# A four-layer graph network on one core: rows padded to 16 bytes, destination tiles in chunks of three at the end, and fusion, loads and stores moved

## The chip, the cores and the metric

One Trainium2 chip; the kernel runs on one of its cores. The metric is device time in microseconds (us) from the first to the last instruction with what lies around them. Three runs of the kernel before gave 3668.65, 3674.61 and 3675.11 us, a median of 3674.61.

## The reference

3327 nodes with 512 features pass through four layers. Every layer normalises its input, clips it at zero, and adds its result to the input. Layers 0 to 2 are graph attention with 8, 4 and 8 heads; layer 1 adds self loops to the mask. Layer 3 averages over neighbours and applies three linear maps.

```python
# layer 0 (layers 1 and 2 alike; 1 with 4 heads of 128)
Wh = jnp.einsum('nd,hdo->hno', x, W)
e = jax.nn.leaky_relu(f1[:, :, None] + f2[:, None, :], negative_slope=ALPHA)
attention = jax.nn.softmax(jnp.where(adj[None] > 0, e, NEG_INF), axis=-1)
out = jax.nn.elu(jnp.einsum('hnm,hmo->hno', attention, Wh))
# layer 3
agg = mask @ x / jnp.maximum(deg, 1.0)
combined = jnp.concatenate([x @ W_self + b_self, agg @ W_nb + b_nb], axis=-1)
out = jax.nn.relu(combined @ W_comb + b_comb)
# every layer
h = jnp.maximum(_layernorm(x, axis=-1), 0.0)
x = x + layer(h, adj, ...)
```

The adjacency matrix is sparse and skewed: its density is about 0.01.

## The kernel before

**Tiles.** The nodes are 26 tiles of 128 rows (the last has 127). Destination tiles are handled in chunks of up to four (`chunks`, `PER`, L64 and L65), so six chunks of four and one of two. Source tiles are loaded in five groups `JG` of 6, 6, 6, 4 and 4 (L67).

**Attention as two masked sums.** The exponential of a leaky ReLU of s1+s2 is one of two products, depending on the sign of s1+s2. So for every head and pair of tiles a gate of zeros and twos is made (L550 on ACT, or L547 on DVE for the tiles in `GP_ON_DVE`), masked by an AND (L556) and turned into its complement by an XOR (L560); TensorE then multiplies each of the two 0/2 masks with one of two "pieces" of the projected features (L588 and L591). To keep float32 accuracy a feature is split into three bf16 parts side by side: 65 columns times 3 is 195. A row of a source tile holds both halves: 196 columns with one column of ones (for the degree), then 195: `AO` is 196 and `HW` 391 in `dims` (L102). Layer 1 has rows of 388 columns for group 0 and float32 pairs of 258 for the other four groups, for which masks are converted first (`real`, L488 and L493). Its rows are not touched by the change.

**Loops.** `attention` (L505) runs over chunks, heads, and passes of two destination tiles; a pass goes over all 26 source tiles. For each head and chunk all pieces are loaded anew (`load_pieces`, L498; L528 in layer 1) by SP. After the passes DVE reduces the sums (L602, L606), scales them and divides (L619 to L626) into tiles `A`, which are finished later: ELU and residual (`finish`, L654: ACT, DVE, POOL), normalisation (`norm`, L280), transposes (`transposed`, L131), projection for the next layer (`project`, L329, or `project_last`, L370, for layer 3), splitting and storing pieces (`pieces`, L298) and sending scores (`send_s1`, L389).

**Hooks.** These steps of finished tiles are stages of a tile (`node_stages`, L397) that `Hooks.run` (L471) slips in after a pass: a new tile after every third pass, in the last chunk after every pass. What is left when the layer ends is drained (L637 to L641). The last tiles of layer 3's first projection are kept in `left` (tiles 22 to 25).

**Fusion.** Layer 3's maps are multiplied together beforehand: `fuse_weights` (L161), four blocks of 128 rows and one product for the biases, at the end of layers 0 and 1, called by `close` after the drain.

**Order.** Buffers rotate (`bufs`): an instruction that writes a buffer waits for the last reader of what was there. Instructions on an engine, and DMAs of a queue, run in the order in which they were placed when the program was built; `after` (L141) asks for a place behind another instruction, without a wait on the chip. That order isn't the order of the lines: the trace shows gates of a new layer on ACT ahead of copies for tiles still being drained. The first passes of a layer leave out the last group of source tiles (L567 to L569), because it contains the drained tiles.

Of the kernel before, what the change touches and what calls it, by code (L numbers as in the profile page):

```python
# [37 lines left out]
P = 128  # L38
# [14 lines left out]
def tile_gnn(ctx: ExitStack, tc: tile.TileContext, x, adj, W0, a01, W1, al, ar, W2, a2,  # L53
# [11 lines left out]
    chunks = [(t, min(PER, NT - t)) for t in range(0, NT, PER)]  # L65
# [29 lines left out]

    xs = [x] + [[dram.tile([n * P, D], F32, name=f"x{l}_{c}") for c, (_, n) in enumerate(chunks)]
# [5 lines left out]
    def dims(l):  # L102

        H = heads[l]
        DA = D // H + 1
        AO = 3 * DA + 1
        return H, DA, AO, (2 * AO - 1 if l != 1 else 2 * AO)

# [38 lines left out]
    gone = []  # L147

# [12 lines left out]
    def fuse_weights(i, wc):  # L161
        w_src, b_src = ((Ws, bs), (Wn, bn))[i]
        b = pre.tile([P, KC], F32, name="bv", bufs=1)
        if i == 0:
            nc.gpsimd.dma_start(bias, bc.partition_broadcast(P))
        with nc.allow_non_contiguous_dma(reason="512 values"):
            nc.gpsimd.dma_start(b, b_src.rearrange("(c p) -> p c", p=P))
        for k in range(KC):
            w = pre.tile([P, D], F32, name="xt")
            nc.gpsimd.dma_start(w, w_src[k * P:(k + 1) * P, :])  # L170
            wT = transposed(w, pre, "hT")
            pw = ps.tile([P, D], F32, name="mm")
            for m in range(KC):
                nc.tensor.matmul(pw, wT[:, m, :], wc[:, m, :], start=(m == 0), stop=(m == KC - 1))
            xo = pre.tile([P, D], F32, name="h")
            nc.scalar.copy(xo, pw)
            nc.gpsimd.dma_start(Xd[i][k * P:(k + 1) * P, :], xo)
        pb = ps.tile([P, D], F32, name="mm")
        for m in range(KC):
            nc.tensor.matmul(pb, b[:, m:m + 1].to_broadcast([P, P]), wc[:, m, :], start=(m == 0), stop=(m == KC - 1))  # L180
        nc.vector.tensor_add(bias, bias, pb)
# [54 lines left out]
    def open_layer(l):  # L236
        L = Layer()
        L.l = l
        if l == 3:
# [40 lines left out]
    def norm(xt, pool):  # L280
# [3 lines left out]
        nc.vector.bn_aggr(mv[:, 0:2], st)  # L284
# [13 lines left out]
    def pieces(L, t, AB, pool, first):  # L298
# [9 lines left out]
        nc.gpsimd.memset(pt[:, :, :, o, 3 * DA:AO] if l == 1 else pt[:, :, o, 3 * DA:AO], 1.0)  # L308
# [14 lines left out]
        if o == two - 1 and l == 1:  # L323
            for a in range(2):
                nc.sync.dma_start(abd[l][g][:, a, :, js, :].rearrange("h p j w -> p h j w"), pt[:, :, a])
        elif o == two - 1:
            stored[t] = nc.sync.dma_start(abd[l][g][:, :, js, :].rearrange("h p j w -> p h j w"), pt).ins.name

    def project(L, t, hT, pool, first):  # L329
# [7 lines left out]
        for f in range(2):  # L337
            pw = (accs if first else ps).tile([P, D // 2 + H], F32, name="acc" if first else "mm")
            for k in range(KC):
                nc.tensor.matmul(pw, hT[:, k, :], L.w[:, k, f, :], start=(k == 0), stop=(k == KC - 1))  # L340
# [13 lines left out]
        if l == 1 and KIND[g] != "b":  # L354
            for f in range(2):
# [5 lines left out]
                nc.sync.dma_start(abd[l][g][hs, :, :, jj, :].rearrange("h a p w -> p h a w"),  # L361
                                  pt.rearrange("p h a s d -> p h a (s d)").bitcast(F32))
# [7 lines left out]
    def project_last(L, t, hT, i):  # L370
# [5 lines left out]
        for k in range(KC):  # L376
            nc.tensor.matmul(pw, hT[:, k, :], L.w[i][:, k, :], start=(k == 0), stop=(k == KC - 1))
        if i == 0:
            y = pre.tile([P, D], F32, name="AB", bufs=1)
            nc.vector.tensor_add(y, pw, bias)  # L380
            nc.sync.dma_start(y1d[c][kk * P:kk * P + n, :], y[:n])
# [7 lines left out]
    def send_s1(L, t, pool, first):  # L389
# [5 lines left out]
        nc.sync.dma_start(s1d[L.l][:, t * P:(t + 1) * P], s1t[:H])  # L395

    def node_stages(L, t, get_x, pool, first=False):  # L397
# [7 lines left out]
        def s1():  # L405
            behind = gone[-1] if gone else None
            q["hT"] = transposed(q["h"], mp, "A", 6, behind) if late else transposed(q["h"], pool, "hT", 2, behind)

# [843 lines left out]
```

## Time and profile before

| what | value |
|---|---|
| profiled execution, its own time | 3671.68 us |
| span of its instructions | 3669.8 us |
| mean granted clock of TensorE | 0.986 |
| PE busy | 3508.7 us (96%) |
| DVE busy | 2651.4 us (72%) |
| ACT busy | 2518.0 us (69%) |
| POOL busy | 589.2 us (16%) |
| DMA | 773.05 MB, 211 GB/s |
| layer 0 attention | 176.9 to 1263.5 us |
| layer 1 attention | 1281.0 to 2156.5 us |
| layer 2 attention | 2184.5 to 3309.4 us |
| aggregation of layer 3 | 3342.6 us to the end |

PE is TensorE's matmuls, PEld its weight loads, DVE the vector engine, ACT the scalar engine, POOL the general-purpose one, SP the engine that issues most DMAs. A row of a group of instructions gives line, engine, operation, tiles written and read, shapes and count, then busy us, mean ns of one (a latency: matmuls overlap), then the engine's idle time before them and what ended it. A row of a stage gives its start and end, its length, busy us of each engine with the count of instructions, then the granted clock, DMA share and rate. A row in order of time gives start, duration, instruction, and in brackets the idle time before it and its releaser.

### The profile page before, as it was taken

Reading aid. Unit: us, or ns where it says so; the run is one execution under the profiler, and the core shown is the slowest. Engines: PE = TensorE matmul, PEld = TensorE weight load, DVE = VectorE, ACT = ScalarE, POOL = GpSimd, SP = SyncE. Lnnn points to the kernel's source line nnn. Section 1 sums busy time; section 2 is a strip of 40 time slices with the busy share of each in tenths; the row PEclk is TensorE's granted clock in tenths of the full one; section 3 lists DMA queues with packets and bytes.
Section 4 is the critical chain, followed back from the end, with each engine's and each line's share of the span. In section 5 each row is a group of like instructions: output and inputs, shape, how many; then the busy total and the mean of one; then the engine's idle time right before and its main releaser. Section 6 shows DMA issues by size and latency. Waiting matters only on the chain. (4 is left out here: it accounts for less than half of the span.)

```text
span 3669.8 us, 78902 instructions
## 1 busy us (share of the span) xinstructions
PE 3508.7 (96%) x31348; PEld 3172.0 (86%) x31348; DVE 2651.4 (72%) x5230; ACT 2518.0 (69%) x4170; POOL 589.2 (16%) x832
## 2 busy tenths in 40 slices
PE   7799999999999899999999979999999999998998
PEld 5599999999999778888888859989898989886886
DVE  7698888888887789888888766767776767672121
ACT  5678787777787779888888656767666767571111
POOL 6501221202010102122223220001010101010000
PEclk9999999999999999999999989999999999999999
DMA  7777677777756877777877876545455554476331
GB/s 210 230 207 226 201 226 212 215 220 224 220 189 215 270 262 262 270 257 249 275 249 261 320 229 188 187 169 189 167 182 167 191 171 171 160 276 238 113 104 51
DMA packets 321402, 773.05 MB, mean 211 GB/s; under 512 B 36037, under 2 KB 143560, under 8 KB 320384
## 3 DMA queue, kind: packets, MB, share of 16 engines
q1 hardware_dynamic: 293920, 707.23, 57.6%
q0 software_dynamic: 27104, 60.69, 6.8%
q8 instruction: 249, 4.08, 0.4%
q14 instruction: 129, 1.06, 0.1%
HBM read 661.25 MB, written 128.68 MB: 215 GB/s over the span
## 5 line engine op out<-in xcount | busy, mean ns | idle before, releaser
L588 PE MATMUL acc<-ab,tht 128*128 128x195 bf16 (+1 forms) x10816 | 1872.8, 248 | 20.9 <-DVE tht L556 14.5
L591 PE MATMUL acc<-ab,gt 128*128 128x195 bf16 (+1 forms) x10816 | 1872.3, 249 | 3.1 <-DVE gt L560 2.3
L550 ACT ACTIVATE gt<-s1b,ks 128x512 fp8e4<-128x512 f32 (+1 forms) x2464 | 1456.5, 677 | 279.0 <-issue 150.4
L588 PEld LDWEIGHTS <-tht 128*128 128x128 fp8e4 x10816 | 1060.0, 98 | 28.0 <-DVE tht L556 15.4
L591 PEld LDWEIGHTS <-gt 128*128 128x128 fp8e4 x10816 | 1052.6, 97 | 26.6 <-issue 14.6
L581 PE MATMUL acc<-ab,t 128*128 128x258 f32 x4160 | 544.6, 289 | 22.7 <-ACT t L493 19.6
L581 PEld LDWEIGHTS acc<-ab,t 128*128 128x128 f32 x4160 | 520.2, 192 | 35.8 <-ACT t L493 23.1
L556 DVE TENSOR_TENSOR tht<-gt,m 128x768 uint32<-128x768 uint32 (+3 forms) x560 | 447.8, 800 | 141.6 <-ACT gt L550 138.8
L560 DVE TENSOR_TENSOR gt<-tht,m 128x768 uint32<-128x768 uint32 (+3 forms) x560 | 447.0, 799 | 8.2
L493 ACT CAST t<-tht 128x1536 fp32r<-128x1536 fp8e4 x208 | 300.7, 1469 | 57.6 <-PE acc L581 47.2
L547 DVE TENSOR_SCALAR gt<-s1b,ns 128x512 fp8e4<-128x512 f32 (+1 forms) x448 | 213.9, 480 | 150.0 <-PE acc L591 138.3
L664 POOL TENSOR_TENSOR xt<-xt,e 128x512 f32<-128x512 f32 x78 | 114.7, 1471 | 1270.8 <-DVE e L663 1230.6
L788 PE MATMUL acc<-y,mf 128*128 128x512 f32 x1352 | 309.8, 391 | 1.3 <-DVE mf L783 1.3
L550 ACT ACTIVATE tht<-s1b,ks 128x512 fp8e4<-128x512 f32 (+1 forms) x504 | 306.9, 679 | 2.0 <-DMA s1b<-s 2.0
L788 PEld LDWEIGHTS acc<-y,mf 128*128 128x128 f32 x1352 | 253.6, 188 | 57.4 <-DVE mf L783 1.7
L606 DVE TENSOR_REDUCE R<-acc 128x130 f32<-128x390 f32 x416 | 214.7, 555 | 81.8 <-PE acc L591 81.7
L584 PE MATMUL acc<-ab,tht 128*128 128x387 bf16 x1248 | 225.5, 329 | 4.6 <-DMA ab<-ab 2.5
L785 ACT CAST mf<-m 128x768 fp32r<-128x768 fp8e4 (+1 forms) x78 | 59.1, 762 | 244.7 <-PE acc L788 232.9
L340 PE MATMUL mm<-w,hT 128*128 128x260 f32 (+1 forms) x832 | 200.3, 393 | 13.2 <-ACT hT L138 10.4
L340 PEld LDWEIGHTS mm<-w,hT 128*128 128x128 f32 x832 | 156.9, 194 | 38.4 <-ACT hT L138 11.2
L584 PEld LDWEIGHTS <-tht 128*128 128x128 fp8e4 x1248 | 118.7, 98 | 81.9 <-DMA ab<-ab 2.9
L319 POOL TENSOR_TENSOR pt<-r 128x520 bf16<-128x520 f32 (+1 forms) x116 | 143.2, 1254 | 266.1 <-DVE r L315 249.3
(132 smaller groups left out, 3138.2 us busy)
## 6 DMA issues: line engine op xcount, KB each, us to landing
ab<-ab SPq DMA_DIRECT2D x336, 586.5 KB
ab<-ab SPq DMA_DIRECT2D x224, 391.0 KB
ab<-ab SPq DMA_DIRECT2D x112, 774.0 KB
ab<-ab SPq DMA_DIRECT2D x112, 516.0 KB
ab<-ab SPq DMA_DIRECT2D x56, 582.0 KB
s1b<-s SPq DMA_DIRECT2D x120, 256.0 KB
m<-mask SPq DMA_DIRECT2D x72, 384.0 KB
ab<-pt SPq DMA_DIRECT2D x40, 516.0 KB
```

Of the source, the lines that this page charges most:

```text
L340: nc.tensor.matmul(pw, hT[:, k, :], L.w[:, k, f, :], start=(k == 0), stop=(k == KC - 1))
L493: (nc.scalar.copy if KIND[g] == "s" else nc.vector.tensor_copy)(t[:, :k1 - k0, :nj], th[a][g][:, k0:k1])
L547: nc.vector.tensor_scalar(gv[:, :, jj, :], s1v, L.ns2[:, j, h:h + 1], 2.0, op0=ALU.is_gt, op1=ALU.mult, saturate=False)
L550: nc.scalar.activation(gv[:, :, jj, :], s1v, AF.Relu, bias=L.ks2[:, j, h:h + 1], scale=BIG, saturate=False)
L556: nc.vector.tensor_tensor(pu, gu, mu, ALU.bitwise_and)
L560: nc.vector.tensor_tensor(gu, pu, mu, ALU.bitwise_xor)
L581: mm = nc.tensor.matmul(acc[k][:, :2 * DA], thr[g][:, k - ks[0], jj, :], ab[a][g][:, jj, :], start=(j == 0), stop=(j == NT - 1), skip_grou ...
L584: mm = nc.tensor.matmul(acc[k][:, :3 * DA], th[a][g][:, k, jj, :], ab[a][g][:, jj, :3 * DA], start=(j == 0), stop=(j == NT - 1), skip_grou ...
L588: nc.tensor.matmul(acc[k][:, :3 * DA + o], th[0][g][:, k, jj, :], ab[0][g][:, jj, :3 * DA + o], start=(j == 0), stop=False, skip_group_che ...
L591: mm = nc.tensor.matmul(acc[k][:, AO - o:HW], th[1][g][:, k, jj, :], ab[0][g][:, jj, AO - o:HW], start=False, stop=(j == NT - 1), skip_gro ...
L606: nc.vector.tensor_reduce(R[:, k], v.rearrange("p a (s d) -> p a d s", s=3), AX.X, ALU.add)
L788: nc.tensor.matmul(acc[k], mf[:, jj, :], y2[g][:, jj, s, :], start=(j0 + jj == 0 and s == 0), stop=(j0 + jj == NT - 1 and s == 1))
```

## The change

- The last six destination tiles are two chunks of three instead of four and two.
- In layers 0 and 2 a half row (`AO`) is rounded up to a multiple of 8 columns, 200, and the row (`HW`) is twice that, 400. The columns 195 to 199 of both halves are filled with ones. The degree is summed from two columns of the accumulator.
- The pieces of layers 1 and 2 are stored by stage s3 instead of s2 (`to_store`); their scores are sent through POOL's queue instead of SP's.
- Tiles `A` have 8, 6 and 8 buffers in layers 0, 1 and 2 instead of 6, 5 and 6, and layer 1's gate tiles 11 instead of 12.
- In the last head of a layer the x rows of the last chunk are loaded into `A` buffers by POOL, and the biases and the first two weight blocks of the fusion are loaded.
- Two blocks of the fusion and its biases come ahead of the drain, two behind it. The additions behind the kept projections come after the drain.
- In the last chunk a new tile is taken up after every second pass.

```diff
-    chunks = [(t, min(PER, NT - t)) for t in range(0, NT, PER)]
+    chunks = [(0, 4), (4, 4), (8, 4), (12, 4), (16, 4), (20, 3), (23, 3)]
...
+    A_BUFS = [8, 6, 8]
...
-        AO = 3 * DA + 1
-        return H, DA, AO, (2 * AO - 1 if l != 1 else 2 * AO)
+        AO = -(-(3 * DA + 1) // 8) * 8 if l != 1 else 3 * DA + 1
+        return H, DA, AO, 2 * AO
...
-    def fuse_weights(i, wc):
...
+    class Fusion:
+        def __init__(self, i, wc):
+            self.i, self.wc, self.w = i, wc, {}
+            self.w_src, self.b_src = ((Ws, bs), (Wn, bn))[i]
+        def load(self, k, behind):
+            self.w[k] = pre.tile([P, D], F32, name="xt")
+            after(nc.gpsimd.dma_start(self.w[k], self.w_src[k * P:(k + 1) * P, :]), behind)
+        def block(self, k, behind):
+            w = self.w.pop(k)
+            wT = transposed(w, pre, "hT", 2, behind)
             pw = ps.tile([P, D], F32, name="mm")
             for m in range(KC):
+                nc.tensor.matmul(pw, wT[:, m, :], self.wc[:, m, :], start=(m == 0), stop=(m == KC - 1))
+            nc.scalar.copy(w, pw)
+            nc.gpsimd.dma_start(Xd[self.i][k * P:(k + 1) * P, :], w)
...
-        nc.gpsimd.memset(pt[:, :, :, o, 3 * DA:AO] if l == 1 else pt[:, :, o, 3 * DA:AO], 1.0)
+        nc.gpsimd.memset(pt[:, :, :, o, 3 * DA:AO] if l == 1 else
+                         pt[:, :, o].rearrange("p h (a w) -> p h a w", a=2)[..., 3 * DA:AO], 1.0)
...
+        elif first and o == two - 1:
+            stored[t] = nc.sync.dma_start(abd[l][g][:, :, js, :].rearrange("h p j w -> p h j w"), pt).ins.name
         elif o == two - 1:
-            stored[t] = nc.sync.dma_start(abd[l][g][:, :, js, :].rearrange("h p j w -> p h j w"), pt).ins.name
+            L.to_store.append((abd[l][g][:, :, js, :].rearrange("h p j w -> p h j w"), pt))
...
-        nc.sync.dma_start(s1d[L.l][:, t * P:(t + 1) * P], s1t[:H])
+        (nc.sync if first else nc.gpsimd).dma_start(s1d[L.l][:, t * P:(t + 1) * P], s1t[:H])
...
             if L.l != 3:
+                for to, pt in L.to_store:
+                    nc.sync.dma_start(to, pt)
+                L.to_store = []
                 send_s1(L, t, pool, first)
...
+                if last and h == H - 1:
+                    for k in range(nt):
+                        x_last[t0 + k] = load_x(l, t0 + k, mp, "A", A_BUFS[l], behind=gone[-1])
+                    fusion = close()
+                    if fusion:
+                        fusion.load_biases()
+                        fusion.load(0, gone[-1])
+                        fusion.load(1, gone[-1])
...
-                    pt = mp.tile([P, PER * JM * P], FP8, name="tht", bufs=12 if l == 1 else 7)
+                    pt = mp.tile([P, PER * JM * P], FP8, name="tht", bufs=11 if l == 1 else 7)
...
-                                    mm = nc.tensor.matmul(acc[k][:, AO - o:HW], th[1][g][:, k, jj, :],
-                                                     ab[0][g][:, jj, AO - o:HW], start=False, stop=(j == NT - 1),
+                                    mm = nc.tensor.matmul(acc[k][:, AO:AO + 3 * DA + o], th[1][g][:, k, jj, :],
+                                                     ab[0][g][:, jj, AO:AO + 3 * DA + o], start=False, stop=(j == NT - 1),
...
-                                nc.vector.tensor_copy(deg2[:n, t0 + k:t0 + k + 1], acc[k][:n, 3 * DA:AO])
+                                nc.vector.tensor_reduce(deg2[:n, t0 + k:t0 + k + 1],
+                                                        acc[k][:n, 3 * DA:AO + 3 * DA + 1:AO], AX.X, ALU.add)
...
-                        hooks.run(1 if last else 3, hook, 2 if hook % 2 and c == 0 or hook % 3 == 0 and c else 1)
+                        hooks.run(2 if last else 3, hook, 2 if hook % 2 and c == 0 or hook % 3 == 0 and c else 1)
...
         hooks.run(1, 0, 0)
-        run_left()
+        fusion = close()
+        if fusion:
+            for k in range(2):
+                fusion.block(k, gone[-1])
+            fusion.biases(gone[-1])
+        adds = run_left()
         hooks.drain()
-        close()
-        run_left()
+        for add in adds:
+            add()
+        if fusion:
+            for k in range(2, KC):
+                fusion.load(k, gone[-1])
+                fusion.block(k, gone[-1])
+        for add in run_left():
+            add()
...
+    def load_x(l, t, pool, *name, behind=None):
+        n = pn(t)
+        xt = pool.tile([P, D], F32, name=name[0], bufs=name[1])
...
+        ld = (nc.gpsimd if behind else nc.sync).dma_start(xt[:n], x_rows(l, t))
```

## The prediction, made before the changed kernel was run

> **What bounds the kernel now.** I read the costliest groups, then busy time stage by stage, then the order of time in the places where TensorE stood still. The chain that ended last reaches only into the final aggregation (PE 8% of the span) and says nothing of the rest. The two groups that cost most, from the page:
>
> ```profile
> L588 PE MATMUL acc<-ab,tht 128*128 128x195 bf16 (+1 forms) x10816 | 1872.8, 248 | 20.9 <-DVE tht L556 14.5
> L591 PE MATMUL acc<-ab,gt 128*128 128x195 bf16 (+1 forms) x10816 | 1872.3, 249 | 3.1 <-DVE gt L560 2.3
> ```
>
> Half of the span is these 21,632 matmuls of 195 columns (layers 0 and 2). Busy time by stage, in this order: layer 0 chunks 1 to 5, its last chunk, the passage to layer 1; layer 1 chunks 1 to 5, its last chunk, the passage to layer 2; layer 2 chunks 1 to 5, its last chunk, the passage to the aggregation:
>
> ```profile
> core 0: us, PE busy (x) PEld busy (x) DVE busy (x) ACT busy (x) POOL busy (x), PEclk, DMA share, GB/s
> ...
> 338.00:1168.00 830.00, 821.53 (x9196) 808.11 (x9195) 683.37 (x1356) 648.53 (x1115) 137.30 (x205) 1.00 0.70 212
> 1168.00:1263.50 95.50, 89.18 (x925) 85.72 (x922) 75.96 (x203) 79.18 (x196) 13.70 (x20) 1.00 0.88 289
> 1263.50:1307.00 43.50, 32.98 (x117) 19.80 (x116) 23.91 (x53) 36.22 (x63) 12.11 (x22) 0.88 0.69 240
> ...
> 1416.00:2071.50 655.50, 636.46 (x4588) 559.42 (x4587) 558.74 (x1015) 540.44 (x749) 163.42 (x178) 0.98 0.76 258
> 2071.50:2156.50 85.00, 75.00 (x502) 62.22 (x500) 62.10 (x138) 53.41 (x92) 26.44 (x31) 0.98 0.95 335
> 2156.50:2212.60 56.10, 35.66 (x147) 22.78 (x147) 29.94 (x51) 33.51 (x61) 16.12 (x23) 0.79 0.65 198
> ...
> 2352.00:3212.00 860.00, 860.00 (x8727) 779.47 (x8725) 603.01 (x1184) 575.55 (x945) 66.01 (x100) 1.00 0.51 174
> 3212.00:3309.40 97.40, 94.38 (x900) 81.84 (x897) 71.48 (x189) 69.75 (x165) 15.98 (x21) 1.00 0.77 267
> 3309.40:3342.60 33.20, 25.01 (x58) 11.03 (x57) 9.42 (x23) 9.31 (x14) 7.84 (x13) 0.85 0.75 303
> ```
>
> TensorE is the bound: length less PE busy is 8.5, 6.3, 10.5, 19.0, 10.0, 20.4, 0.0, 3.0 and 8.2 us. So time is won by shorter matmul steps, or out of these gaps. The last chunks (two tiles) load as many pieces as full ones: DMA share 0.88 and 0.95 against 0.70 and 0.76. In the passages the granted clock is 0.88, 0.79 and 0.85. The passage to layer 2, in order of time:
>
> ```profile
> 2166.53 1.12 PE L134 MATMUL tp<-ident,h 128*128 128x128 f32 x4 [10.00 <-ACT h L289]
> ...
> 2171.63 1.26 POOL L664 TENSOR_TENSOR xt<-xt,e 128x512 f32<-128x512 f32 x1 [6.00 <-DMA xt<-x]
> ...
> 2175.52 1.33 ACT L550 ACTIVATE gt<-s1b,ks 128x512 fp8e4<-128x512 f32 x2 [9.04 <-DMA s1b<-s]
> ...
> 2176.76 0.56 ACT L138 COPY hT<-tp 128x512 f32<-128x512 f32 x1
> ...
> 2177.37 3.01 PE L340 MATMUL mm<-w,hT 128*128 128x264 f32 x6 [9.73 <-ACT hT L138]
> ```
>
> TensorE waits 10.0 us for the first tile's normalisation and 9.7 us for a copy queued on ACT behind gates that wait for a row of scores. A gap of the kind that repeats in layer 1, chunks 1 to 5:
>
> ```profile
> 1718.82 1.14 ACT L317 COPY pt<-AB 128x520 bf16<-128x520 bf16 x2
> ...
> 1719.87 1.47 ACT L493 CAST t<-tht 128x1536 fp32r<-128x1536 fp8e4 x1
> ...
> 1721.38 0.86 PE L581 MATMUL acc<-ab,t 128*128 128x258 f32 x5 [3.44 <-ACT t L493]
> ```
>
> **The change, part by part.**
>
> *Padded rows.* I took each step from one L588/L591 start to the next: 21,364 lie between 80 and 92 ns, mean 85.67, and they are sorted. Layer 1's matmuls of 387 columns step 163.3 ns at the shortest, these of 195 step 83.3: 192 columns more take 80.0 more, 2.4 columns per ns, so 195 alone would be 81.3 and 83.3 is 200. The 196 columns of layer 0's first head take the same 83.3. It looks as if whole groups of 8 elements (16 bytes) were read. Rows lie 391 elements apart, 7 past a multiple of 8, so the start moves with j. The second matmul of a pair starts 391j+196 in: at j=4, 10, 16 a multiple of 8, and it takes 83.8; at j=3, 9, 15 one past, 83.8 to 85; elsewhere 87 to 88. Layer 1's 387-column matmuls take 168.3 for the first of a pair at odd j (4 past) and 163.3 at even j. One row does not fit: the first matmul of the second tile of a pair takes 83.4 wherever it starts. With rows of 400 and halves at 200 all start at multiples. Price per step 85.67−83.8=1.87; times 21,632, 40 us. Ends: 0 (the pattern is not one of addresses) and 51 (all at 83.3); I take the row of an aligned matmul. No cover can swallow it where TensorE is never idle (2352 to 3212).
>
> The Trainium skill (TensorE: Matmul & The Clock Gate, "Back-to-back issue gap") gives columns over 2.4 plus 2.5 ns for a warm matmul and names no address, so 83.75 for every one of these. The rows of 87 and 88 contradict it; by that rule padding, which leaves 195 columns, would give nothing, and the sum below would be 45.
>
> Its price: rows 2.3% longer in 560 loads, hidden under TensorE at a DMA share of 0.51 to 0.76. The fill at L308 grows from 8 to 80 elements (0.13 us; bound above by the 0.20 of a 128x128 fill) 52 times on an idle POOL: 4 us, hidden. The degree becomes a reduction of two columns, 26 times, 0.15 us up to 0.44 (a reduction of 208) each on DVE: 8 us at most, hidden at 683 of 830 us.
>
> *Chunks of 3 and 3.* Matmul count is unchanged; ACT gates step 613 ns at 512 columns and 399 at 256, so 506 at 384: two threes cost what four and two do. Layer 1 gets 32 more conversions (L493), 16 on ACT at a fixed 0.19 us: 3 us, hidden. Layer 1 loads 6.5 MB a head, now over some 25 us instead of 21: 259 GB/s, what the middle chunks sustain. The three gaps are 6.3+10.0+3.0=19; ends 5 and 19; I take 13, as chunks of three still have only 3/4 of the cover. Hooks run every second pass where a head has twice the passes: the same rate.
>
> *Buffers, moved stores.* With five A buffers in layer 1 a chunk's fourth tile waits until the old chunk's third is finished, which is in head 1; DVE's normalising of head 0 so stretches from L619 at 1711.3 to L626 at 1721.1, and casts and reductions queue with it. With six it waits for the second, in head 0. SP's piece stores (L327) wait 139 us on ACT in all with piece loads queued behind; issuing them a stage later removes that. Late is then the store of the drained tiles' pieces, which only the last group's loads follow; the first passes of the next layer leave that group out, and cover 4x22x0.13=11 us (layer 1) or 4x44x0.0857=15 us (layer 2). The score stores (L395) move to POOL, where an issue costs 0.6 us (L665): 52 of them, 31 us on an engine busy 16%; there they queue behind L664, but only the next layer reads them. Gate buffers in layer 1 fall from 12 to 11; a head uses five. Of 19.0 idle I take 9; ends −5 and 17.
>
> *Passages.* Before, two drained tiles, then four fusion blocks and the biases. After: two blocks and biases (2×4.1+3.5, from 8 steps of 0.43 and 4 of 0.11) on TensorE while the first tile is normalised, then three tiles at 4.3 (16×0.222 and transposes), then two blocks: 11.8+12.9+8.2=33. Against 43.5 less 2.8 of attention (17 matmuls of 0.163) plus the 4.3 of the tile that no longer sits in the chunk: 12 in the best case. But those loads and the x rows now go through POOL, which stands still before this passage:
>
> ```profile
> 1264.12 0.36 POOL L225 COPY m<-dg 128x32 uint32<-128x32 uint32 x2 [52.86 <-DVE R L606]
> ```
>
> If they are queued behind it they land some 5 us later (x stores: 5.1 median). Ends 3 and 12; I take 9. To layer 2: 56.1 less 4.0 of attention plus 4.3, less 33, is 23. The x row that came 15 us after its issue at 2155.9 is loaded early; the ACT copy may still stand behind gates waiting for s1b (9.0). Ends 9 and 23; I take 14. To the aggregation no fusion exists; one projection (3.5) instead of two covers the 14 us of normalising (3309.4 to 3323.35), then three tiles at 7.4 and 3 us of half clock: 40 against 33.2+7.4. Ends −6 and 6; I take 0.
>
> Sum 40+13+9+9+14+0=85. The profiled execution took 3671.7 us (span 3669.8 and 1.9 around it), 2.9 under the median 3674.6 and inside the runs. So 3674.6−85=3589.6; I say 3590.
>
> **Rivals.**
> *The passages do not fill* (order on ACT and POOL keeps the blocks late): the 23 of the two passages is lost: 3613. For it: 9.04 and 52.86 above; against: the fusion weights depend on nothing in the layer.
> *Padding does nothing*: 45 remain, 3630. For it: the odd row of 83.4; against: the steps sort by j, in two shapes.
> *Everything pays*: 51+19+17+12+23+6=128, 3547.
> *Slower*: eleven gate buffers starve layer 1, each of 28 heads standing as at 1721 (3.4 us): 95 lost against 85, so 3685. It decides from 85/28=3.0 us a head. Against: ten buffers hold two heads.
>
> **How the numbers follow.** Forecast 0.59 (own range 3560 to 3613), passages 0.17, padding 0.13, everything 0.05, slower 0.04, and 0.02 that gains and losses cancel. 3550 to 3636 leaves out the slower case, the cancelling one and the two tails: under 2 in 10. 0.2% (7 us) is about what a measurement of this kernel tells from no change: faster 0.94, same 0.02, slower 0.04.
>
> **What would show it.** Right: L588 steps of 83 to 84 ns at all j and layer 2's heads without hooks at 17.4 us instead of 17.8; L174 between the last attention matmul and the first L134 of h; PE idle in the last chunks under 6 us together; granted clock above 0.9 in the first two passages. Wrong: steps still sorted into 83 and 87; a releaser DMA ab in layer 0's chunks, L493 waits at every head of layer 1, or POOL queues before L664 in the passages.

## The result and the profile after

The changed kernel takes 3648.11 us (median of 5, 3646.87 to 3657.41) against 3671.61 (median of 5, 3668.56 to 3675.11): a ratio of 0.9942, 95% interval 0.9927 to 0.9957. That is 23.5 us less where 85 were forecast, and 12 us outside the range. The profiled execution took 3648.11 us (span 3646.2).

The costliest groups on the page of the changed kernel (L631 and L634 are the matmuls of layers 0 and 2, before L588 and L591; L624 is layer 1's, before L581):

```profile
L631 PE MATMUL acc<-ab,tht 128*128 128x195 bf16 (+1 forms) x10816 | 1844.1, 248 | 18.1 <-DVE tht L599 13.0
L634 PE MATMUL acc<-ab,gt 128*128 128x195 bf16 (+1 forms) x10816 | 1843.8, 248 | 11.2 <-ACT gt L593 5.9
...
L624 PE MATMUL acc<-ab,t 128*128 128x258 f32 x4160 | 549.1, 290 | 44.8 <-ACT t L527 29.6
```

Layer 1's group on the page of before:

```profile
L581 PE MATMUL acc<-ab,t 128*128 128x258 f32 x4160 | 544.6, 289 | 22.7 <-ACT t L493 19.6
```

The two big groups are 57 us shorter in sum, but a matmul of 248 ns starts every 84, so the two overlap and their sum counts time twice: by the steps, 84.16 ns against 85.67, they save 32 us. Part of that is paid back as waits: idle before L634 grew from 3.1 to 11.2 us, and before layer 1's matmuls from 22.7 to 44.8. Busy time by stage of the changed kernel, in the order of before (for each layer all chunks but the first and the last, the last chunk, the passage):

```profile
core 0: us, PE busy (x) PEld busy (x) DVE busy (x) ACT busy (x) POOL busy (x), PEclk, DMA share, GB/s
330.50:1121.50 791.00, 774.74 (x8775) 759.52 (x8772) 662.45 (x1334) 627.57 (x1108) 148.52 (x221) 1.00 0.74 224
1121.50:1244.10 122.60, 119.59 (x1315) 117.01 (x1314) 93.62 (x212) 97.19 (x194) 17.68 (x30) 0.99 0.67 234
1244.10:1287.00 42.90, 38.01 (x140) 23.44 (x139) 25.68 (x58) 32.36 (x58) 13.86 (x24) 0.92 0.55 179
1394.80:2045.30 650.50, 612.17 (x4374) 535.41 (x4372) 539.93 (x999) 524.62 (x746) 168.21 (x197) 0.98 0.72 258
2045.30:2150.90 105.60, 98.56 (x691) 84.43 (x690) 83.47 (x165) 69.87 (x105) 24.60 (x34) 0.98 0.84 311
2150.90:2192.00 41.10, 34.26 (x148) 22.32 (x147) 26.77 (x48) 30.12 (x58) 19.82 (x28) 0.96 0.41 141
2333.80:3151.10 817.30, 814.52 (x8307) 733.23 (x8305) 587.57 (x1164) 555.79 (x937) 67.28 (x100) 1.00 0.54 184
3151.10:3276.30 125.20, 123.96 (x1303) 113.78 (x1301) 95.85 (x205) 86.23 (x167) 13.40 (x20) 1.00 0.60 211
3276.30:3320.30 44.00, 32.17 (x69) 13.76 (x69) 11.59 (x27) 12.36 (x19) 11.43 (x18) 0.81 0.74 287
```

Length less PE busy is now 16.3, 3.0, 4.9, 38.3, 7.0, 6.8, 2.8, 1.2 and 11.8 us: 92 in all against 86 before. So TensorE stands still as long as before. The last chunks (19.3 to 11.2) and the first two passages (30.9 to 11.7) won what layer 1's middle chunks (19.0 to 38.3), layer 0's (8.5 to 16.3) and the last passage (8.2 to 11.8) lost.

For a comparison of like with like I cut the traces at the same instructions: chunks from their first attention matmul, a passage from the last attention matmul to the second head of the next layer (or to the aggregation's first matmul). Chunks are counted from one here and in the expectations (the prediction counts from zero). In us, before and after:

| stage | before | after | change |
|---|---|---|---|
| start and first projections | 176.9 | 170.3 | -6.6 |
| layer 0, chunks 1 to 5 | 832.4 | 824.4 | -8.0 |
| layer 0, last 6 tiles | 254.2 | 249.5 | -4.7 |
| passage to layer 1 | 69.0 | 67.2 | -1.8 |
| layer 1, chunk 1 without its first head | 84.1 | 83.5 | -0.6 |
| layer 1, chunks 2 to 5 | 524.5 | 536.2 | +11.7 |
| layer 1, last 6 tiles | 215.5 | 219.9 | +4.4 |
| passage to layer 2 | 70.1 | 59.2 | -10.9 |
| layer 2, chunks 1 to 5 | 813.5 | 801.7 | -11.8 |
| layer 2, last 6 tiles | 269.4 | 264.5 | -4.9 |
| passage to the aggregation | 33.1 | 44.0 | +10.9 |
| aggregation | 327.2 | 325.9 | -1.3 |

They sum to 23.6. The first row I did not forecast; other kernels with the same start show 170 to 174, so the 176.9 of the one profile of before may be chance.

### The profile page after: what moved, and what is told of

Read it like the earlier page. It is cut to its first block, busy times and chain, and to the rows that moved or that the text cites. A ratio compares the mean times of both kernels' runs of the same rounds, so it can differ in the third digit from the quotient of the medians.

```text
span 3646.2 us, 78928 instructions
## 1 busy us (share of the span) xinstructions
PE 3485.7 (96%) x31348; PEld 3143.3 (86%) x31348; DVE 2667.6 (73%) x5243; ACT 2522.5 (69%) x4186; POOL 619.9 (17%) x896
## 4 chain that ended last, share of the span: by engine, by line
PE 44%; DVE 7%; ACT 4%; POOL 3%; issue 3%; DMA 1%; SPq 0%; POOLq 0%; DVEq 0%; ACTq 0%
PE acc L634 12%; PE acc L631 12%; PE acc L854 8%; PE mm L399 5%; PE acc L624 4%; ACT tht L593 2%; PE acc L627 1%; PE mm L362 1%; POOL xt L730 1%; DVE tht L599 1%; ACT t L527 1%; DVE tht L590 1%; DVE t L527 1%; DVE tht L659 1%; DVE R L645 1%
## 5 line engine op out<-in xcount | busy, mean ns | idle before, releaser
L631 PE MATMUL acc<-ab,tht 128*128 128x195 bf16 (+1 forms) x10816 | 1844.1, 248 | 18.1 <-DVE tht L599 13.0
L634 PE MATMUL acc<-ab,gt 128*128 128x195 bf16 (+1 forms) x10816 | 1843.8, 248 | 11.2 <-ACT gt L593 5.9
L593 ACT ACTIVATE gt<-s1b,ks 128x512 fp8e4<-128x512 f32 (+1 forms) x2464 | 1456.4, 677 | 252.9 <-issue 150.1
L634 PEld LDWEIGHTS <-gt 128*128 128x128 fp8e4 x10816 | 1060.7, 98 | 36.2 <-issue 15.4
L631 PEld LDWEIGHTS <-tht 128*128 128x128 fp8e4 x10816 | 1061.0, 98 | 26.5 <-DVE tht L599 14.2
L624 PE MATMUL acc<-ab,t 128*128 128x258 f32 x4160 | 549.1, 290 | 44.8 <-ACT t L527 29.6
L624 PEld LDWEIGHTS acc<-ab,t 128*128 128x128 f32 x4160 | 521.9, 192 | 61.3 <-ACT t L527 34.9
L590 DVE TENSOR_SCALAR gt<-s1b,ns 128x512 fp8e4<-128x512 f32 (+1 forms) x448 | 233.1, 525 | 114.8 <-PE acc L634 114.4
L730 POOL TENSOR_TENSOR xt<-xt,e 128x512 f32<-128x512 f32 x69 | 106.6, 1546 | 1157.6 <-DVE e L729 1128.1
L362 PE MATMUL mm<-w,hT 128*128 128x260 f32 (+1 forms) x832 | 196.6, 390 | 1.8 <-DVE AB L373 1.1
L527 DVE CAST t<-tht 128x1024 fp32r<-128x1024 fp8e4 x224 | 146.3, 658 | 53.4 <-PE acc L624 53.1
```

What stands on the lines that cost most here:

```text
L362: L.mm = nc.tensor.matmul(pw, hT[:, k, :], L.w[:, k, f, :], start=(k == 0), stop=(k == KC - 1)).ins.name
L527: (nc.scalar.copy if KIND[g] == "s" else nc.vector.tensor_copy)(t[:, :k1 - k0, :nj], th[a][g][:, k0:k1])
L590: nc.vector.tensor_scalar(gv[:, :, jj, :], s1v, L.ns2[:, j, h:h + 1], 2.0, op0=ALU.is_gt, op1=ALU.mult, saturate=False)
L593: nc.scalar.activation(gv[:, :, jj, :], s1v, AF.Relu, bias=L.ks2[:, j, h:h + 1], scale=BIG, saturate=False)
L624: mm = nc.tensor.matmul(acc[k][:, :2 * DA], thr[g][:, k - ks[0], jj, :], ab[a][g][:, jj, :], start=(j == 0), stop=(j == NT - 1), skip_grou ...
L631: nc.tensor.matmul(acc[k][:, :3 * DA + o], th[0][g][:, k, jj, :], ab[0][g][:, jj, :3 * DA + o], start=(j == 0), stop=False, skip_group_che ...
```

## The experiments

Each set of runs was timed with the kernel before beside it, whose median wandered from 3669 to 3680 us between sets; so the ratios are what compares. Of the kernel before, 0.001 is 3.7 us.

| run | us | ratio to before | 95% interval |
|---|---|---|---|
| changed kernel | 3648.11 | 0.9942 | 0.9927 to 0.9957 |
| pad_only | 3638.11 | 0.9918 | 0.9902 to 0.9935 |
| pad_392 | 3655.54 | 0.9940 | 0.9924 to 0.9957 |
| chunks_42 | 3626.03 | 0.9882 | 0.9865 to 0.9898 |
| gates12_a5 | 3647.20 | 0.9937 | 0.9920 to 0.9954 |
| stores_now | 3651.67 | 0.9951 | 0.9934 to 0.9967 |
| c42_g12_a5 | 3620.09 | 0.9834 | 0.9818 to 0.9851 |
| c42_g11_a5 | 3626.45 | 0.9854 | 0.9837 to 0.9870 |
| c42_g13_a4 | 3620.14 | 0.9839 | 0.9823 to 0.9855 |
| c42_fuse_late | 3662.18 | 0.9948 | 0.9930 to 0.9965 |
| c42_x_late | 3636.37 | 0.9876 | 0.9858 to 0.9894 |
| third_pt | 3649.28 | 0.9919 | 0.9902 to 0.9936 |
| masks_later | 3619.21 | 0.9837 | 0.9820 to 0.9853 |
| l0_dve_1 | 3616.82 | 0.9830 | 0.9813 to 0.9846 |
| l0_dve_5 | 3613.17 | 0.9821 | 0.9804 to 0.9837 |

**Padding alone (pad_only).** The kernel before with this:

```diff
-        AO = 3 * DA + 1
-        return H, DA, AO, (2 * AO - 1 if l != 1 else 2 * AO)
+        AO = -(-(3 * DA + 1) // 8) * 8 if l != 1 else 3 * DA + 1
+        return H, DA, AO, 2 * AO
...
```

> The kernel before with the padded rows alone (halves at 200, rows of 400, borders filled, the degree as a reduction of two columns); chunks, buffers, stores and passages as before. Theory A, alignment: every attention matmul of layers 0 and 2 steps about 84.2 ns instead of 85.7, as in the changed kernel, so 21,632 x 1.5 = 32 us are taken off TensorE, and with TensorE the bound all of it comes off the time: about 3640. Theory B, layer 0 is nearly bound by ScalarE and VectorE: the steps fall all the same, but about half of layer 0's 16 us comes back as waits for gates, so about 24 us: 3648. Rival C, the shorter steps of the changed kernel come from something else than the rows: steps stay at 85.7 and the time at 3672. Layer 1 from its second chunk on should stay as before within 2 us in all three.

Measured: 31.3 us less than before. Steps of 80 to 92 ns have a mean of 84.16 ns in both layers (85.7 before). The padding alone is worth more than the whole change (the intervals overlap a little), and what else was changed costs some 8 to 9 us in sum. Theory A holds for the total. In layer 0 B is partly right too: its chunks 1 to 5 gained 5.9 us, though their 20/26 of 10,816 x 1.5 ns are 12.5.

That the total meets theory A is in part luck. Cut by stage as above, only 18 of the 32 us that separate the two profiles lie where the steps became shorter: 5.0 in layer 0 and 12.9 in layer 2. The start gave 5.3, the passages 4.6, and layer 1, whose rows are not padded, 4.6 (its chunks 2 to 5 took 521.2 us, not within 2 of 524.5). No run tells whether these belong to the padding or to the one profile of before.

**Rows of 392 (pad_392).** As above with one line undone:

```diff
-        AO = -(-(3 * DA + 1) // 8) * 8 if l != 1 else 3 * DA + 1
+        AO = 3 * DA + 1
```

> The kernel before with rows of 392 and halves at 196: every first matmul of a pair then starts at a multiple of 8 elements and every second one 4 past. Theory A, the start address sets the step: 84 ns for the first, 87 to 88 for the second of the first tile as the rows of before that start 4 past (88): 10,816 x about 1.5 to 3.7 us come back of what the full padding gave, so about half of its gain: 3650 to 3656 where the full padding gave 3638. Rival B, what costs is the odd row length or the shared column, not the start: 84 everywhere and 3638. Rival C, whole groups of 8 elements are read: 4 past and 195 columns touch 25 groups as from the start: 84 everywhere too.

Measured: 3655.54 us. That lies in theory A's range, but the range was set beside a kernel before of 3669 us, and here it took 3679. As a ratio the range is 0.9947 to 0.9963; 0.9940 was measured, and its interval overlaps this range and the full padding both. So the time does not decide, and the steps do: their mean is 85.07 ns, 0.6 ns under that of before where the rows of 400 give 1.5. The mean steps by place in the row, over layer 2, in ns, worked out from the trace (j is the place in its group of source tiles):

```
matmul of a pair          rows of 391 (by j)   rows of 392   rows of 400
first,  first tile        83.9 to 88.3         83.3 to 83.4  84.2
second, first tile        83.3 to 88.0         86.7 to 87.0  84.2
first,  second tile       83.3 to 84.8         83.3          84.2
second, second tile       83.4 to 87.7         86.7 to 87.0  84.2
```

The same 195 columns step 83.3 ns from a multiple of 8 elements and 87 from 4 past one. In rows of 392 only second matmuls start 4 past, but the rows of 391 part the start from the place in the pair: there the second matmul of the first tile takes 83.3 from a multiple of 8 and 88.0 from 4 past, and the first takes 83.9 and 88.3. So it is the start. One row stays outside this, as the prediction noted: the first matmul of the second tile takes 83.3 to 84.8 from any start, and no run tells why. The row length is ruled out, and so is my picture of whole groups of 8 being read: 4 past, 195 columns touch 25 groups, as they do from the start. The rule of the Trainium skill that I weighed (TensorE: Matmul & The Clock Gate, "Back-to-back issue gap": columns over 2.4 plus 2.5 ns, by estimate 83.75 for 195 columns, with no address in it) fits the aligned rows within 0.5 ns and fails for those 4 past by 3. The section gives this rule for an isolated matmul and has other figures for a stream of weight loads and matmuls, as this kernel runs; the prediction took the rule for the stream.

**The last chunk of two (chunks_42).** The changed kernel with:

```diff
-    chunks = [(0, 4), (4, 4), (8, 4), (12, 4), (16, 4), (20, 3), (23, 3)]
+    chunks = [(t, min(PER, NT - t)) for t in range(0, NT, PER)]
...
-                        hooks.run(2 if last else 3,
+                        hooks.run(1 if last else 3,
```

> The changed kernel with the last chunk of two tiles again (4, 4, 4, 4, 4, 4, 2) and one hook a pass there; all else as changed. Theory A, the threes cost time at the ends: the third drained tile makes the passage to the aggregation longer (before 360.5 us from the end of layer 2's attention, changed 370.2) and layer 1's last seven tiles longer (215.1 and 219.5); both come back, 10 to 14 us: about 3636. Rival B, as I forecast: the threes gain the 13 us of idle time in the last chunks, so undoing them costs that much: about 3661. Rival C, both are about equal: 3648 within 4.

Measured: 3626.03 us; the threes, with the rate of hooks that goes with them, cost 22 us. By stage, threes against two: last 6 tiles 249.5 and 250.0, 219.9 and 218.2, 264.5 and 265.5, so the same; passages 67.2 and 61.7, 59.2 and 54.3, 44.0 and 27.5, in sum 27 us. The idle time won in the last chunk returns in the sixth, which has three tiles instead of four: over the three layers TensorE stands still for 11.2 us in the last chunks instead of 16.3, and for 18.5 in the sixth instead of 6.9. And the third drained tile is on the path in all three passages.

**The third tile at the aggregation (third_pt).** The changed kernel with:

```diff
-            pt = pre.tile([P, 2, D], F32R, name="pt")
+            pt = pre.tile([P, 2, D], F32R, name="r", bufs=1) if t == NT - 1 else pre.tile([P, 2, D], F32R, name="pt")
```

> The changed kernel with the last tile's converted product (pt of L416 to L418) in a buffer of its own, that the layers before used for r, instead of the second turn of two buffers. Theory A, of the 11 us that the passage to the aggregation lost, 4 to 6 are the wait of that tile for the first tile's store (9.6 us idle on ScalarE before L416, then 3.75 on TensorE): the passage takes 38 to 40 us instead of 44 and the time 3642 to 3645. Rival B, the wait is hidden behind TensorE, whose projections run at half clock there: 43 to 44 and 3648. In both the rest of the loss belongs to the third tile's own matmuls.

The end of the changed kernel's passage, in order of time:

```profile
3309.45 0.59 ACT L416 CAST pt<-mm 128x512 fp32r<-128x512 f32 x1 [9.57 <-DMA y<-pt]
...
3310.81 10.07 PE L399 MATMUL mm<-w,A 128*128 128x512 f32 x16 [3.75 <-DVE pt L417]
...
3320.31 1.02 PE L854 MATMUL acc<-y,mf 128*128 128x512 f32 x2
```

The third tile's copy waits 9.57 us for a store that was issued at 3295.3 us, because there are two buffers for three tiles. With a buffer of its own:

```profile
3312.56 14.00 PE L399 MATMUL mm<-w,A 128*128 128x512 f32 x32 [0.62 <-ACT A L141]
...
3326.00 1.26 PE L854 MATMUL acc<-y,mf 128*128 128x512 f32 x3
```

The passage falls from 44.0 to 37.0 us: 3.75 of idle time, and the 16 matmuls behind it, which took 10.07 us after the pause and take 7 without it. The granted clock of the passage is 0.86 instead of 0.81. In the total this is not separated: 3649.28 us, a ratio 0.0023 (8 us) lower, but its interval overlaps that of the changed kernel. So the place is shown, the gain in the time is not.

**Layer 1's buffers (gates12_a5).** The changed kernel with:

```diff
-    A_BUFS = [8, 6, 8]
+    A_BUFS = [8, 5, 8]
...
-                    for k in range(nt):
+                    for k in range(min(nt, A_BUFS[l] - nt)):
...
-                    pt = mp.tile([P, PER * JM * P], FP8, name="tht", bufs=11 if l == 1 else 7)
+                    pt = mp.tile([P, PER * JM * P], FP8, name="tht", bufs=12 if l == 1 else 7)
```

> The changed kernel with layer 1's buffers as before: twelve gate buffers and five of A (so only two of the last three x rows are loaded early there). Theory A, the buffers cause layer 1's new waits (chunks 2 to 5 take 536 us against 524.5 before, with a wait of 3 to 4 us on L527 in the third head): they fall back to about 525 and the time to about 3637. Rival B, the later issue of the stores causes them: 536 stays and the time is 3646 to 3650.

Measured: chunks 2 to 5 of layer 1 take 525.9 us instead of 536.2, as A says; but the total stays at 3647.2, because with five A buffers only two of the three x rows could be early, and the passage to layer 2 went from 59.2 to 70.3: in it POOL waits 13.0 us for the load of the third row, and DVE 14.1 us for POOL.

**The same with the last chunk of two (c42_g12_a5).** Both edits together; the two x rows then fit.

> The changed kernel with the last chunk of two again, and layer 1 with twelve gate buffers and five of A. Theory A, the two losses found are separate and both come back: layer 1's chunks 2 to 5 at 525 us as with the buffers of before, the passages and last chunks as in the run with the last chunk of two (62, 54, 28 us): 3626 less 10, about 3616. With two tiles at the end five A buffers still hold both early x rows, so the passage to layer 2 should not grow to 70 us as it did with three. Rival B, the two overlap (the third tile and layer 1's waits compete for the same ScalarE time): 3622 or more.

Measured: 3620.09 us, between A and B; by the ratio, 0.0048 (18 us) under the run with the last chunk of two, it is more than A's 10. The kernel before differs by 8 us between these two sets, so the stages decide: layer 1 523.5, passages 61.7, 54.5 and 27.5. The losses add up, as A says.

**Gates or A (c42_g11_a5).** The same with the gate buffers at 11 again.

> The same with eleven gate buffers and five of A: tells the gate buffers from the A buffers. Theory A, the gate buffers: with eleven ScalarE runs less far ahead, and layer 1's chunks 2 to 5 stay at about 535 us: 3626. Rival B, the sixth A buffer: VectorE no longer stands at the normalising of the first head, so the tile stages fall on other passes; with five the chunks take about 525 us even with eleven gates: 3616.

Measured: layer 1's chunks 2 to 5 take 535.0 us. It is the gate buffers; the A buffers do nothing there (534.7 with six). The group of layer 1's matmuls in these two runs, first with twelve gates, then with eleven:

```profile
L624 PE MATMUL acc<-ab,t 128*128 128x258 f32 x4160 | 545.4, 290 | 22.1 <-ACT t L527 20.9
```

```profile
L624 PE MATMUL acc<-ab,t 128*128 128x258 f32 x4160 | 546.3, 290 | 36.6 <-ACT t L527 30.7
```

Over all kernels that I profiled, eleven gates give 534 to 538 us for these chunks (7 profiles) and twelve or thirteen 519 to 526 (9). What the wait looks like in the changed kernel, in order of time, in the third head of a chunk:

```profile
1590.86 5.10 PE L624 MATMUL acc<-ab,t 128*128 128x258 f32 x40
...
1591.58 4.39 ACT L593 ACTIVATE tht<-s1b,ks 128x512 fp8e4<-128x512 f32 x7
...
1596.07 2.54 ACT L593 ACTIVATE tht<-s1b,ks 128x512 fp8e4<-128x512 f32 x4
...
1598.52 1.14 ACT L337 COPY pt<-AB 128x520 bf16<-128x520 bf16 x2
...
1599.56 1.46 ACT L527 CAST t<-tht 128x1536 fp32r<-128x1536 fp8e4 x1
...
1601.08 1.70 PE L624 MATMUL acc<-ab,t 128*128 128x258 f32 x12 [3.04 <-ACT t L527]
```

ScalarE is busy throughout; the conversion that TensorE needs next stands behind eleven gates of a later head and a tile's copy. The two kernels with eleven and twelve gates have the same instructions in the same order on TensorE and another order on VectorE and ScalarE: one buffer less changes which gates are placed ahead of which conversions.

**One more gate (c42_g13_a4).** The same with 13 gates and four A.

> The run with the last chunk of two, with thirteen gate buffers and four of A in layer 1. Theory A, each gate buffer more lets ScalarE and VectorE run further ahead: layer 1's chunks 2 to 5 fall from 535 (eleven) and 523.5 (twelve) to 510 to 518, and the time to 3608 to 3614. Rival B, twelve are enough: 521 to 526, 3616 to 3621. Rival C, with four A buffers a chunk's first tile waits for the old chunk's first tile to be finished, and VectorE stands at the normalising of the first head: 530 or more, 3626 or more.

Measured: layer 1 525.0, 3620.14 us. Twelve are enough (rival B).

**The stores (stores_now).** The changed kernel with, in all three places, the store in the stage that makes the pieces, and the scores on SP:

```diff
-            L.to_store.append((abd[l][g][:, :, js, :].rearrange("h p j w -> p h j w"), pt))
+            nc.sync.dma_start(abd[l][g][:, :, js, :].rearrange("h p j w -> p h j w"), pt)
...
-        (nc.sync if first else nc.gpsimd).dma_start(s1d
+        nc.sync.dma_start(s1d
```

> The changed kernel with the stores where they were before: the pieces are stored by SyncE in the stage that makes them, the scores by SyncE too. Theory A, the buffers cause layer 1's new waits: chunks 2 to 5 of layer 1 stay at about 536 us and the time within 4 us of 3648. Rival B, the moved stores cause them: about 525 and 3637. My forecast put a gain on the moved stores (up to half of 9 us): then this one is slower than 3648, by about 4.

Measured: layer 1 536.3 us, as with the moved stores; 3651.67, a difference of 3.5 us that the intervals do not separate. The moved stores neither caused layer 1's loss nor gained anything there.

**The order of the fusion (c42_fuse_late).** The run with the last chunk of two, and:

```diff
-        if fusion:
-            for k in range(2):
-                fusion.block(k, gone[-1])
-            fusion.biases(gone[-1])
         adds = run_left()
         hooks.drain()
...
-            for k in range(2, KC):
-                fusion.load(k, gone[-1])
+            for k in range(KC):
+                if k > 1:
+                    fusion.load(k, gone[-1])
                 fusion.block(k, gone[-1])
+            fusion.biases(gone[-1])
```

> The changed kernel with the last chunk of two, and all four fusion blocks and the biases behind the two drained tiles instead of two and the biases ahead of them (their loads stay early). Theory A, the two blocks and biases ahead of the tiles cover the normalising of the first tile (about 10 us) in both passages to layers 1 and 2: without them each is 5 to 10 us longer, 67 to 72 instead of 61.7 and 59 to 64 instead of 54.3: together 3636 to 3646. Rival B, the gain of the passages came from the early x rows and loads and not from the order: both within 2 us, 3626.

Measured: 3662.18 us, 36 more, or 24 by the ratios; passages 76.1 and 70.8 instead of 61.7 and 54.3. Above A's ranges. The two passages with the blocks ahead of the tiles (chunks_42), and behind them:

```profile
1252.20:1314.00 61.80, 57.78 (x310) 42.20 (x309) 39.96 (x80) 51.31 (x79) 12.87 (x24) 0.94 0.71 243
2150.70:2205.00 54.30, 47.40 (x308) 34.73 (x307) 36.57 (x63) 41.73 (x75) 15.99 (x23) 0.97 0.62 223
```

```profile
1248.80:1324.90 76.10, 59.70 (x309) 43.25 (x308) 43.73 (x88) 56.52 (x87) 13.87 (x24) 0.89 0.61 201
2164.20:2234.90 70.70, 51.64 (x307) 37.54 (x308) 36.39 (x63) 42.14 (x75) 16.11 (x23) 0.86 0.52 178
```

The work is the same (some 309 matmuls each), idle time is 16.4 and 19.1 instead of 4.0 and 6.9, and the granted clock 0.89 and 0.86 instead of 0.94 and 0.97. The old wait for the first tile is back, and the matmuls behind it take longer (16 of L362 in 6.50 us, in the changed kernel 15 in 4.55):

```profile
2174.15 1.12 PE L137 MATMUL tp<-ident,h 128*128 128x128 f32 x4 [10.00 <-ACT h L308]
2175.95 6.50 PE L362 MATMUL mm<-w,hT 128*128 128x264 f32 x16 [0.68 <-ACT hT L141]
```

In the changed kernel the fusion stands where that wait was:

```profile
2152.04 7.13 PE L181 MATMUL mm<-w,hT 128*128 128x512 f32 x16 [0.24 <-ACT hT L141]
...
2159.01 3.60 PE L195 MATMUL mm<-w,bv 128*128 128x512 f32 x8
...
2162.44 0.60 PE L137 MATMUL tp<-ident,h 128*128 128x128 f32 x4
...
2166.85 1.11 PE L137 MATMUL tp<-ident,h 128*128 128x128 f32 x4 [3.81 <-ACT h L308]
2167.76 4.55 PE L362 MATMUL mm<-w,hT 128*128 128x264 f32 x15
```

**The early x rows (c42_x_late).** The run with the last chunk of two, with:

```diff
-                    for k in range(nt):
-                        x_last[t0 + k] = load_x(l, t0 + k, mp, "A", A_BUFS[l], behind=gone[-1])
...
-        xt = x_last.pop(t) if t in x_last else load_x(l, t, pre, "xt", 2)
+        xt = load_x(l, t, mp, "A", A_BUFS[l]) if t >= chunks[-1][0] else load_x(l, t, pre, "xt", 2)
```

> The changed kernel with the last chunk of two, and the last two x rows of each layer issued on SyncE when their tile is finished instead of early on GpSimd. Theory A, the early x rows gave the passage to layer 2 most of what it gained (before, that row landed 15 us after its issue): that passage is 5 to 10 us longer than 54.3, those to layer 1 (61.7) and to the aggregation (27.5) 0 to 4 each: 3631 to 3642. Rival B, the two fusion blocks cover the row either way: all within 2 us, 3626.

Measured: the passage to layer 2 is 3.8 us longer (58.1), that to layer 1 the same, that to the aggregation 1.7 shorter; the ratios overlap. Less than A says: where two blocks stand ahead of the tiles, most of the row's lateness is covered.

**Layer 0 (masks_later, l0_dve_1, l0_dve_5).** In the padded kernels the first, fifth, sixth and seventh heads of layer 0's chunks 2 to 5 fall by 1.8, 1.0 to 1.2, 1.3 and 1.2 us (sums over four chunks) in every kernel with rows of 400 that I cut up so, except masks_later, which moves masks between heads. The second to fourth heads (264.6 us in all before) do not fall, they grow: 268.6, 265.6, 270.2 and 272.5 in pad_only, the changed kernel, chunks_42 and c42_g12_a5. Three attempts on c42_g12_a5:

```diff
-                        hooks.run(1 if last else 3, hook, 2 if hook % 2 and c == 0 or hook % 3 == 0 and c else 1)
+                        hooks.run(1 if last else 3, hook, 2 if hook % 2 and c == 0 or 8 <= hook < 14 and c else 1)
```

> The run with the last chunk of two, twelve gates and five A (3620), with the second mask tile of a hook in layer 0 made in heads 5 to 7 of a chunk instead of at every third hook. Theory A, layer 0's second and third heads kept none of the shorter steps (22.6 to 22.7 and 20.9 to 21.0 to 22.7 us with the padding alone, where the other heads fell by 0.3 to 0.4) because VectorE makes masks and finishes tiles there together: with fewer masks there these two fall by 0.3 to 1.5 us a head, 3 to 10 us over chunks 2 to 5. Rival B, the finishing of tiles alone fills them: within 1 us in these chunks.

Measured: 3619.21 us. The third head falls by 14.7 us, the sixth and seventh grow by 14.0, and the four chunks stay (673.4 and 673.9): the masks' time moved with them. The traces show one part of it. In heads two to four of these chunks TensorE is idle for 7.9 us before the change and for 11.4, 11.8 and 11.6 in pad_only, the changed kernel and c42_g12_a5; all of the 7.9, and 9.3 to 10.2 of the others, stands before the transposes that make masks (L220 in the changed kernel), which wait for loads of adjacency rows and for DVE. So idle time grew by 3.5 to 3.9 us, 1.4 to 2.3 of it there, about as much as the steps of 2,496 matmuls saved in these heads (3.7). With the masks moved, 3.7 us of idle time are left in them.

```diff
-GP_ON_DVE = [(5, 12, 19),
+GP_ON_DVE = [(12,),
```

> The run with the last chunk of two, twelve gates and five A (3620), with one of 26 gates of a head on VectorE in layer 0 instead of three (two more on ScalarE). Theory A, VectorE makes layer 0's second to fourth heads give back the shorter steps (it makes the masks and finishes the tiles there; heads 2 to 4 of chunks 2 to 5 took 92.1, 89.1 and 91.3 us in all, 272.5, against 264.6 in the kernel before): with 0.5 us x 2 x 4 less on it per chunk row these heads fall by 3 to 8 us over the four chunks: about 3614. Rival B, ScalarE does: it takes 2 x 0.61 us more a head, the heads grow by 5 us or more: 3625 or more. Rival C, neither: within 2 us.

```diff
-GP_ON_DVE = [(5, 12, 19),
+GP_ON_DVE = [(4, 9, 14, 19, 24),
```

> The same with five of 26 gates on VectorE in layer 0 (two fewer on ScalarE). Theory A, VectorE is what gives the steps back: the second to fourth heads grow by 5 us or more over chunks 2 to 5, 3625 or more. Rival B, ScalarE is: they fall by 3 to 8 us, about 3614. Rival C, neither: within 2 us, 3620.

Measured: 3616.82 and 3613.17 us; heads 2 to 4 at 269.5 and 270.3 us, both slightly below 272.5, and within the spread of the others. More or less load on either engine gives no opposite signs, so neither engine's amount of work in gates sets these heads. Layer 0's chunks 1 to 5 spread from 824 to 834 us among padded kernels. Why these heads grow, beyond that idle time, stays open.

## Why the prediction was wrong

The direction was right; the sum was 61 us too high. By the terms of the sum:

**Padded rows: 40 forecast, 31 measured.** The mechanism held, and its rival (padding does nothing) is ruled out. The term was mis-sized in its step: I took 83.8 ns from an aligned matmul, and when all are aligned they take 84.16, so 1.5 ns times 21,632 is 32. That part "no cover can swallow" was right where I said so: layer 2's heads without hooks fell from 17.8 to 17.5 us. That the total came so near to 32 is in part luck, since layers 0 and 2 show only 18 of it.

**Chunks of 3 and 3: 13 forecast, a loss of 22 measured.** This is the largest error. The idle time of the last chunks fell nearly as forecast (19.3 to 11.2 us, not under 6). The equal work behind "two threes cost what four and two do" held for ScalarE (its gates of layers 0 and 2 take 1456.4 us, before 1456.5). What failed is the step from it to a gain, "The three gaps are 6.3+10.0+3.0=19": the sixth chunks, now of three tiles, stand idle for 18.5 us where they stood for 3.8, so the last six tiles took 733.9 us in all, and 733.7 with the last chunk of two. And the third tile cost 27 us in the passages. I had priced it at 4.3, 4.3 and 7.4 and set that off against the chunk that the tile leaves, which did not become shorter for it; the first two came to 5.5 and 4.9, the last to 16.5, 7.0 of it through a wait that no term had: a third tile in a rotation of two buffers behind a store.

**Buffers and moved stores in layer 1: 9 forecast, a loss of 10 to 12 measured.** Neither the sixth A buffer nor the later stores gain anything there. Having eleven gate buffers instead of twelve is the whole loss in these chunks. I named it as the slower rival and put it aside with "ten buffers hold two heads". The mechanism of that rival was right; it cost 0.6 us a head (10.3 over 16 heads), not 3.4. The error is to have let it be all or nothing: the lower end of this term, -5, had been the place for it.

**Passages: 9, 14 and 0 forecast; 1.8, 10.9 and -10.9 measured.** With two tiles at the end they are 7.3, 15.8 and 5.6: 23 for the first two, as forecast (one tile more in the passage and one less in the chunk had cancelled in that sum). So the covering by fusion blocks was right (without it 31 us are lost), the granted clock is above 0.9 in both (0.92 and 0.96), and the rival "the passages do not fill" is wrong. The third tile took the rest back.

**What no term had.** In layer 0 the second to fourth heads of a chunk kept none of the shorter steps: TensorE's idle time in them grew by 3.5 to 3.9 us, about what the steps saved there, 1.4 to 2.3 of it before the transposes that make masks. The longer idle time before L634 (from 3.1 to 11.2 us) is not theirs: in chunks 2 to 5 of layer 0 it is 0.8 us. It stands mostly in the first chunk of that layer and in the sixth and seventh. The prediction took layer 0 as bound by TensorE from 8.5 us of idle time in 830, an average over heads of which some had no slack.

The changed kernel with the last chunk of two and twelve gates (c42_g12_a5, 0.9834) beats the changed kernel and the padding alone; with five gates on VectorE in layer 0 it has the lowest ratio measured, 0.9821 (0.9804 to 0.9837), which does not separate from it.

## What to carry to other kernels

Cost every part of a change in every stage that it passes through: three tiles at the end of a layer looked like a question of the last chunk, and were paid for in the passages. A buffer count that seems sufficient by counting heads may still change the order in which a planner places work on other engines; take a small loss there into the sum, not only a large one into a rival. Where a stream of short matmuls makes up most of the time, look early at their steps by the start of the rows that they read.

## What was not expected of the hardware

With half of the matmuls aligned, these step 83.3 ns; with all aligned, each takes 84.2. So something sets 84.2 that is not the start of the row, and it does not show where a slower matmul alternates with an aligned one. No run here tells what. After 3.75 us without work TensorE took 10.07 us for 16 matmuls that take 7 in an unbroken stream; the granted clock is 0.50 in the first 4 us of them, and 1.00 in the last 3.
